# Long convolution and expert layer on one core: last block's second expert product by slices of 256 channels, first loads in quarters by k, product of the spectra with a third buffer

## Chip, cores and metric

One core of one Trainium2 chip. The metric is device time in microseconds (us) of one execution. The profile of one execution gives its span, from the first to the last instruction; the device time of that execution is a little longer.

## What is computed

A sequence of 8192 tokens with 512 channels, all in float32, goes through a gated long convolution with a residual and a layer norm, and then through an expert layer with a residual and a layer norm:

```
u = x @ W_in + b_in                       # 512 -> 1536
uc = short_conv(u, short_w, short_b)      # three taps per channel
x0, x1, v = split(uc, 3)
v = v * x1                                # the gate
k = gen_filter(8192, W1 .. b3)            # a small net with sines, times exp(-t * delta)
v = causal_fft_conv(v, k, filter_bias)    # rfft of both, product, irfft
y = (v * x0) @ W_out + b_out
x = layernorm(x + y)

logits = grouped @ controller + tie       # groups of 32 tokens, 32 experts, 4 sets
perm = (logits == max over the group's tokens)
dispatched = einsum(bgtd,bgtes->bgesd)
inner = relu(einsum(bgesd,desf->bgesf) + bias)      # f = 32
intermediate = einsum(bgesf,esfd->bgesd)            # the second expert product
out = einsum(bgesd,bgtes->bgtd)                     # back to the tokens
x = layernorm(x + out)
```

## The kernel before

**Stages.** `project` computes u, the short convolution and the gate, and the filter taps beside it; `convolve` does the long convolution as a Fourier transform written as matrix products; `experts` does the output projection, the first norm, the expert layer and the second norm. A scheduler orders the instructions of each engine by an estimate and puts in the waits; in `experts` TensorE's order is the one written down.

**Projection.** Tokens are taken in 16 blocks of 512 (`xt`, four tiles of 128 input channels, index k), output channels in four tiles `ct`, each with three streams s (x0, x1, v). `load_win(0)` (L153) brings the first channel tile's weights with one DMA per k, then `load_tokens(0)` (L158) brings `xt` with one DMA of 1 MB; SyncE issues both, and after them the small tables and the other channel tiles' weights. `projection` (L244) runs for each s four products over k into one PSUM bank (L256); ScalarE evicts the bank (L259) and VectorE goes on.

**Convolution.** It runs for each of four channel tiles: `over_n1` for taps and gate; `over_n2` (L360), whose 32 groups of four k1 values each make a PSUM tile `px` of two banks and multiply the spectra of taps and gate; `back_over_k2` (L395), 16 groups of four channels into a PSUM tile `pz` of two banks; `back_over_k1` (L415), products `py`. The product of the spectra is: ScalarE copies the taps' half of px to `hs` (L381), VectorE makes two products of 128x512 (`t`, L384, and `hs` in place, L388), and GpSimd subtracts and adds (L392, L393) into the spectrum. `hs` and `t` have two buffers each. The first product of `back_over_k2` needs all 32 groups. Each pz tile is copied by VectorE (L413) and ScalarE (L411) into `z`, and the first py product needs all of z.

**Experts.** Four blocks of 2048 tokens, each in two halves u. `front` makes projection, norm and choice of the next block, piece by piece between other work; `dispatch` and `inner` make the inner activations `h`. `outer` (L672) makes the second product for a half u and 128 channels c: eight expert groups q, four sets s and four quarters r, each a product with 32 rows, 32 columns and 128 channels (`pi`, L691), into pairs of PSUM banks; weights come in DMAs of 512 KB into six buffers `f`; ScalarE copies each pair (L700) into a staging tile, and VectorE turns it by 32x32 blocks (L704, two per call of `outer`). `back` (L710) multiplies the turned tile with the choice (`pc`, L716, 32 calls) and VectorE adds to the residual `x1` (L721). `finish` (L734) makes the second norm of a half: statistics and root on VectorE, normalisation on ScalarE (L760) and stores. In the last half of the last block, statistics are taken per 128 channels right after each addition (L729). PSUM has four pairs (`pair`), tag `x1` has four buffers of 16 KB per partition, tag `big` two of 32 KB.

The loop of the last part calls `outer` for (u, c), and after the next `outer` the `back` of the one before:

```
for u in range(2):
    for c in range(NCT):
        outer(b, u, c, [0]) ...
        turned = outer(b, u, c, [1]) ...
        if last:
            back(*last)
        if u == 1 and c == 0:
            ends = finish(b, 0)
        if u == 1:
            some(ends, 3)
        last = (b, u, c, turned)
```

Of the kernel before, what the change touches and what calls it, by code (L numbers as in the profile page):

```python
# [13 lines left out]
F32 = mybir.dt.float32  # L14
# [18 lines left out]
R = 4  # L33
EQ = E // R
EPS = 1e-5

# [107 lines left out]
def project(tc, i, bank, load, between, kept):  # L144
# [4 lines left out]
    with tc.tile_pool(name="pr1", bufs=1) as hp, tc.tile_pool(name="pr2", bufs=2) as wk:  # L149
# [14 lines left out]

        load_win(0)
        xt = load_tokens(0)
        pe = load(hp, "pe")
# [76 lines left out]
        def projection(b, ct):  # L244
            u = wk.tile([P, 3, TB + 2], F32, tag="u", name=f"u_{ct}_{b}")
            nc.gpsimd.tensor_copy(u[:, :, 0:2], carry[:, ct])
            got = []
            for s in range(3):

# [3 lines left out]

                ps = bank(f"pu_{ct}_{b}_{s}")
                for k in range(NCT):
                    nc.tensor.matmul(  # L256
                        ps, win[ct][:, k, s, :], xt[:, k, :], start=(k == 0), stop=(k == NCT - 1)
                    )
                nc.scalar.activation(u[:, s, 2:], ps, AF.Identity, bias=ch(0))  # L259
                o = wk.tile([P, TB], F32, tag=f"o{s}", name=f"o{s}_{ct}_{b}")  # L260
# [55 lines left out]
def convolve(tc, i, banks, kept, wk, tables, between, y_dram):  # L316
# [9 lines left out]
    with tc.tile_pool(name="cv", bufs=1, reuse_waits="tile") as hp:  # L326
# [33 lines left out]
        def over_n2(ct, both, of_taps, spec):  # L360
            for g in range(N1 // KC):
# [8 lines left out]
                for j in range(KC):  # L370
# [8 lines left out]

                hs = wk.tile([P, 2, 64, KC], F32, tag="hs", name="hs" + nm)  # L380
                nc.scalar.copy(hs, ps[:, :, of_taps].rearrange("p j r c -> p r c j"))  # L381
                d = ps[:, :, 1 - of_taps].rearrange("p j r c -> p r c j")
                t = wk.tile([P, 2, 64, KC], F32, tag="t", name="t" + nm)
                nc.vector.tensor_tensor(  # L384
                    t, d, hs[:, 0:1].to_broadcast([P, 2, 64, KC]), ALU.mult
                )

                nc.vector.tensor_tensor(  # L388
                    hs, d, hs[:, 1:2].to_broadcast([P, 2, 64, KC]), ALU.mult
                )  # L390
                o = spec[:, :, :, g * KC : (g + 1) * KC]
                nc.gpsimd.tensor_tensor(o[:, 0], t[:, 0], hs[:, 1], ALU.subtract)  # L392
                nc.gpsimd.tensor_tensor(o[:, 1], t[:, 1], hs[:, 0], ALU.add)  # L393

        def back_over_k2(ct, spec):  # L395
            for c0 in range(0, 64, CB):
                ps = banks(f"pz_{ct}_{c0}").rearrange("p (h c n) -> p h c n", h=2, c=CB)
                for c in range(CB):
                    for r in range(2):
                        for h in range(2):  # L400
# [5 lines left out]
                            )  # L406
                for h in range(2):
                    o = z[:, :, h * 64 + c0 : h * 64 + c0 + CB]
                    v = ps[:, h].rearrange("p c n -> p n c")
                    if h:  # L410
                        nc.scalar.copy(o, v)  # L411
                    else:
                        nc.vector.tensor_copy(o, v)  # L413

# [43 lines left out]
def experts(tc, i, load, ident, y_dram, out):  # L458
# [11 lines left out]
    with (  # L470
# [239 lines left out]
        def back(b, u, c, turned):  # L710
# [11 lines left out]
            if very_last(b, u):  # L722
# [5 lines left out]
                for t in range(HT):  # L728
                    nc.vector.bn_stats(b.st[:, t, c, :], x1[:, t, :])  # L729

        def very_last(b, u):
            return b.n == NBLK - 1 and u == 1
# [67 lines left out]
        for b in blocks:  # L800
# [23 lines left out]
            ]  # L824
            for u in range(2):
                for c in range(NCT):
                    fa, amid, fb, behind = slots[u * NCT + c]
                    outer(b, u, c, [0])
                    fa(amid)
                    turned = outer(b, u, c, [1])  # L830
                    fb(behind)
# [7 lines that stand above are left out]
# [7 lines left out]
            else:  # L846
                back(*last)
            ends = finish(b, 1)
# [3 lines left out]
def laid_out(a):  # L852
# [13 lines left out]
    for h in range(2):  # L866
# [23 lines left out]

        "f2": m["f2"].reshape(R, EQ // 2, 2, S, F, NCT, P).transpose(5, 1, 0, 4, 2, 3, 6)
        .reshape(NCT, EQ // 2, P, 2 * S * P),
        "ebias": m["bias"].reshape(R, EQ, S, F).transpose(0, 3, 1, 2).reshape(P, EQ * S),
    }
# [19 lines left out]
```

## Time and profile before

| | |
|---|---|
| device time, median of 3 runs | 2342.98 us (2339.41 to 2345.3) |
| profiled execution, device time | 2338.82 us |
| its span | 2337.0 us |
| TensorE busy | 2160.5 us (92%) |
| VectorE, ScalarE, GpSimd busy | 1288.6, 822.6, 479.4 us |
| granted TensorE clock, mean of the span | 0.966 |

The profile names a group by line, engine, operation, and tile (written<-read). PE is TensorE's products, PEld its weight loads, DVE is VectorE, ACT ScalarE, POOL GpSimd, SPq SyncE's DMA issues. A line of the timeline has start, length, engine, line, operation, tiles, shape and count, and in brackets how long the engine had been idle and what ended that. "issue" there is a wait for nothing that the profile shows. In the view of stretches each engine has its busy time and, in brackets, its number of instructions; the clock is the share of TensorE's full speed that was granted. The costliest groups of the page that concern the places above:

```profile
L691 PE MATMUL pi<-f,h 32*32 32x128 f32 x8192 | 140.8, 297 | 51.0 <-issue 29.3
...
L402 PE MATMUL pz<-c_back_sb,place 64*128 64x128 f32 x2048 | 124.7, 284 | 19.0 <-POOL place L392 19.0
```

Columns: busy time and mean ns of one, then idle time before the group and what ended most of it.

### The profile page before, as it was taken

To read this page: it belongs to the slowest core of one execution; us is meant where nothing else is said; L and a number is where in the kernel's file an instruction comes from. 1 tells how busy PE (TensorE), PEld (TensorE's weight loads), DVE (VectorE), ACT (ScalarE), POOL (GpSimd) and SP (SyncE) were. 2 spreads that over 40 slices of the span, in tenths; PEclk is the share of its full clock that TensorE was granted. 3 is DMA by queue.
4 is the path that set the end of the run, shared out by engine and by line. 5 is a ranking of instruction groups with operands and counts; after the bars stand their busy time and mean duration, and the time that the engine had idled before them with its cause. 6 is when DMAs were issued, how large, how long until landed. Compare 5 with 4: busy or idle time off the path is not lost.

```text
span 2337.0 us, 67762 instructions
## 1 busy us (share of the span) xinstructions
PE 2160.5 (92%) x30688; PEld 1487.9 (64%) x30688; DVE 1288.6 (55%) x1852; ACT 822.6 (35%) x1240; POOL 479.4 (21%) x583
## 2 busy tenths in 40 slices
PE   8999999999999999999999998889988999898765
PEld 3444444444446999999999998355555556555644
DVE  4777654454554553453463463466566666656546
ACT  4444555555553321321321321121342243234323
POOL 1111233333331340240250160211101100110000
PEclk9999999999999999999999999999998999899887
DMA  4222224231324645655554564426654664665364
GB/s 144 81 68 65 83 64 162 86 139 59 140 63 164 207 170 193 198 190 186 189 206 172 173 239 159 153 82 208 207 178 142 227 203 131 200 200 182 118 228 147
DMA packets 197016, 362.74 MB, mean 155 GB/s; under 512 B 79084, under 2 KB 118898, under 8 KB 193650
## 3 DMA queue, kind: packets, MB, share of 16 engines
q1 hardware_dynamic: 194424, 341.63, 44.4%
q10 hardware_dynamic: 2304, 16.78, 1.8%
q8 instruction: 241, 3.95, 0.7%
q14 instruction: 47, 0.39, 0.0%
HBM read 274.47 MB, written 83.89 MB: 153 GB/s over the span
## 4 chain that ended last, share of the span: by engine, by line
PE 77%; DVE 9%; ACT 5%; issue 3%; POOL 3%; DMA 1%; SPq 0%; ACTq 0%; POOLq 0%; DVEq 0%
PE pu L256 29%; PE pa L349 9%; PE po L537 8%; PE pz L402 5%; PE py L427 5%; PE pi L691 4%; PE pc L716 3%; PE px L373 3%; PE pl L574 3%; PE pd L621 3%; PE ph L654 2%; POOL place L392 2%; DVE si L704 2%; ACT x L760 2%; POOL place L393 2%
## 5 line engine op out<-in xcount | busy, mean ns | idle before, releaser
L256 PE MATMUL pu<-xt,win 128*128 128x512 f32 x1536 | 673.7, 596 | 11.0 <-DMA xt<-in_xT 11.0
L256 PEld LDWEIGHTS pu<-xt,win 128*128 128x128 f32 x1536 | 289.3, 190 | 370.1 <-issue 349.7
L262 DVE SCALAR_TENSOR_TENSOR o<-u,chan_sb,o 128x512 f32<-128x512 f32 x192 | 144.8, 754 | 296.4 <-ACT o L261 295.5
L537 PE MATMUL po<-wout,yt 128*128 128x512 f32 x512 | 241.8, 616 | 19.7 <-DVE x L541 18.5
L373 PE MATMUL px<-place,tab 128*64 128x128 f32 x4096 | 227.6, 273 | 2.1 <-ACT place L356 1.5
L373 PEld LDWEIGHTS px<-place,tab 128*64 128x64 f32 x4096 | 226.1, 136 | 3.1 <-ACT place L356 2.2
L349 PE MATMUL pa<-c_in_sb,vk 128*64 128x128 f32 x4096 | 224.9, 273 | 2.2 <-ACT place L356 1.6
L349 PEld LDWEIGHTS pa<-c_in_sb,vk 128*64 128x64 f32 x4096 | 223.5, 137 | 3.8 <-ACT place L356 1.8
L700 ACT COPY si<-pi 128x1024 f32<-128x1024 f32 x128 | 123.8, 1013 | 258.3 <-PE pi L691 179.8
L535 POOL TENSOR_TENSOR xt<-xt,b_outb_sb 128x512 f32<-128x512 f32 x64 | 82.4, 1288 | 619.0 <-DMA xt<-in_x 550.8
L704 DVE STREAM_TRANSPOSE si<-si 128x2048 f32<-128x2048 f32 x64 | 144.2, 2289 | 113.0 <-ACT si L700 113.0
L259 ACT ACTIVATE u<-pu,chan_sb 128x512 f32<-128x512 f32 x192 | 130.8, 681 | 188.1 <-PE pu L256 186.4
L392 POOL TENSOR_TENSOR place<-t,hs 128x256 f32<-128x256 f32 x128 | 93.6, 732 | 473.9 <-DVE hs L388 404.6
L691 PE MATMUL pi<-f,h 32*32 32x128 f32 x8192 | 140.8, 297 | 51.0 <-issue 29.3
L537 PEld LDWEIGHTS po<-wout,yt 128*128 128x128 f32 x512 | 94.8, 195 | 131.0 <-issue 96.8
L691 PEld LDWEIGHTS pi<-f,h 32*32 32x32 f32 x8192 | 106.9, 107 | 92.9 <-issue 54.6
L261 ACT ACTIVATE o<-u,chan_sb 128x512 f32<-128x512 f32 x192 | 155.7, 812 | 6.6
L358 DVE COPY place<-pa 128x1024 f32<-128x1024 f32 x64 | 78.3, 1225 | 139.7 <-PE pa L349 135.2
L356 ACT COPY place<-pa 128x1024 f32<-128x1024 f32 x64 | 64.7, 1013 | 251.6 <-PE pa L349 245.6
L402 PE MATMUL pz<-c_back_sb,place 64*128 64x128 f32 x2048 | 124.7, 284 | 19.0 <-POOL place L392 19.0
L402 PEld LDWEIGHTS pz<-c_back_sb,place 64*128 64x128 f32 x2048 | 123.2, 199 | 20.6 <-POOL place L392 19.9
L231 ACT ACTIVATE ex<-delta_sb,negt_sb 128x128 f32<-128x128 f32 x256 | 87.6, 390 | 133.0 <-POOL taps L238 133.0
(79 smaller groups left out, 2532.2 us busy)
## 6 DMA issues: line engine op xcount, KB each, us to landing
f<-in_f SPq DMA_DIRECT2D x192, 512.0 KB, 5.1
tab<-in_c_mid SPq DMA_DIRECT2D x64, 512.0 KB, 3.7
place<-in_c_out SPq DMA_DIRECT2D x64, 512.0 KB, 4.9
xt<-in_xT SPq DMA_DIRECT2D x16, 1024.0 KB, 5.4
x<-o SPq DMA_DIRECT2D x64, 256.0 KB, 2.4
gate<-gate SPq DMA_DIRECT2D x64, 256.0 KB, 2.6
taps<-taps SPq DMA_DIRECT2D x4, 4096.0 KB, 11.2
vk<-taps SPq DMA_DIRECT2D x32, 512.0 KB, 3.8
```

Source lines behind the costliest of these rows:

```text
L256: nc.tensor.matmul(ps, win[ct][:, k, s, :], xt[:, k, :], start=(k == 0), stop=(k == NCT - 1))
L259: nc.scalar.activation(u[:, s, 2:], ps, AF.Identity, bias=ch(0))
L261: nc.scalar.activation(o, u[:, s, 2:], AF.Identity, bias=ch(1), scale=ch(4))
L262: nc.vector.scalar_tensor_tensor(o, u[:, s, 1 : 1 + TB], ch(3), o, ALU.mult, ALU.add)
L349: nc.tensor.matmul(ps[r * 64 : (r + 1) * 64, c * N1 : (c + 1) * N1], vk[:, half * 8 + c, :], cin[:, r, :], start=True, stop=True,)
L373: nc.tensor.matmul(ps[h * 64 : (h + 1) * 64, j, :, r, :], tab[:, g % 2 * KC + j, r * 64 : (r + 1) * 64], both[:, :, g * KC + j, h * 64 : ( ...
L392: nc.gpsimd.tensor_tensor(o[:, 0], t[:, 0], hs[:, 1], ALU.subtract)
L402: nc.tensor.matmul(ps[:, h, c, :], spec[rows, r, c0 + c, :], cback[rows, r].rearrange("p q n -> p (q n)"), start=(r == 0), stop=(r == 1),)
L537: nc.tensor.matmul(ps, got["y"][:, ct, t % 2 * P : (t % 2 + 1) * P], wout[:, ct, :], start=(ct == 0), stop=(ct == NCT - 1),)
L691: nc.tensor.matmul(pss[r // 2][s * T : (s + 1) * T, col : col + P], b.h[rows, at + q, s, u * T : (u + 1) * T], f2[rows, q, s, :], start=Tr ...
L700: nc.scalar.copy(o, pss[rr].rearrange("p (r q d) -> p r d q", r=2, q=4))
L704: nc.vector.transpose(turned[:, d].rearrange("p d g -> p (d g)"), stage[:, d].rearrange("p d e -> p (d e)"),)
```

## The change

Three places. The first weights and tokens are loaded in pairs by k, and the first channel tile's twelve products of the first token block run by k instead of by stream. The product of the spectra becomes a function with three `hs` buffers; the last of the 32 groups is done in two halves of two k1 values, with the addition on VectorE instead of GpSimd, and the last pz tile is copied in two halves. In the last block `outer` is replaced by `wide`: products over 256 channels with the weights in another layout (`f2w`, same bytes), one staging tile of 256 channels, and two turned tiles per call from the buffers of tag `x1`; the two `back` of a call run after the next call.

```diff
+W = 256
...
-        load_win(0)
-        xt = load_tokens(0)
+
+        xt = wk.tile([P, NCT, TB], F32, tag="xt", name="xt_0")
+        for k in range(NCT):
+            nc.sync.dma_start(
+                out=win[0][:, k],
+                in_=i["W_in"].rearrange("(k p) (s t c) -> k t p s c", p=P, s=3, c=P)[k, 0],
+            )
+            nc.sync.dma_start(out=xt[:, k], in_=i["xT"][k * P : (k + 1) * P, 0:TB])
...
+            pss = [bank(f"pu_{ct}_{b}_{s}") for s in range(3)]
+            steps = [(s, k) for s in range(3) for k in range(NCT)]
+            if b == 0 and ct == 0:
+                steps.sort(key=lambda sk: sk[1])
+            for s, k in steps:
+                nc.tensor.matmul(
+                    pss[s], win[ct][:, k, s, :], xt[:, k, :], start=(k == 0), stop=(k == NCT - 1)
+                )
             for s in range(3):
...
-                ps = bank(f"pu_{ct}_{b}_{s}")
-                for k in range(NCT):
-                    nc.tensor.matmul(
-                        ps, win[ct][:, k, s, :], xt[:, k, :], start=(k == 0), stop=(k == NCT - 1)
-                    )
-                nc.scalar.activation(u[:, s, 2:], ps, AF.Identity, bias=ch(0))
+                nc.scalar.activation(u[:, s, 2:], pss[s], AF.Identity, bias=ch(0))
...
-                hs = wk.tile([P, 2, 64, KC], F32, tag="hs", name="hs" + nm)
...
+                n = 2 if g == N1 // KC - 1 else 1
+                for j0 in range(0, KC, KC // n):
+                    product(ps[:, j0 : j0 + KC // n], of_taps, spec, g * KC + j0, n == 2, nm)
+
+        def product(ps, of_taps, spec, k1, short, nm):
+
+            kc = ps.shape[1]
+            hs = wk.tile([P, 2, 64, kc], F32, tag="hs", name=f"hs{nm}_{k1}", bufs=3)
+            nc.scalar.copy(hs, ps[:, :, of_taps].rearrange("p j r c -> p r c j"))
+            d = ps[:, :, 1 - of_taps].rearrange("p j r c -> p r c j")
+            t = wk.tile([P, 2, 64, kc], F32, tag="t", name=f"t{nm}_{k1}")
+            nc.vector.tensor_tensor(t, d, hs[:, 0:1].to_broadcast([P, 2, 64, kc]), ALU.mult)
+
+            nc.vector.tensor_tensor(hs, d, hs[:, 1:2].to_broadcast([P, 2, 64, kc]), ALU.mult)
+            o = spec[:, :, :, k1 : k1 + kc]
+            nc.gpsimd.tensor_tensor(o[:, 0], t[:, 0], hs[:, 1], ALU.subtract)
+            add = nc.vector if short else nc.gpsimd
+            add.tensor_tensor(o[:, 1], t[:, 1], hs[:, 0], ALU.add)
...
-                for h in range(2):
-                    o = z[:, :, h * 64 + c0 : h * 64 + c0 + CB]
-                    v = ps[:, h].rearrange("p c n -> p n c")
...
+                n = 2 if c0 == 64 - CB else 1
+                for c1 in range(0, CB, CB // n):
+                    for h in range(2):
+                        at = h * 64 + c0 + c1
+                        o = z[:, :, at : at + CB // n]
+                        v = ps[:, h, c1 : c1 + CB // n].rearrange("p c n -> p n c")
...
+        def wide(b, u, c):
+
+
+            stage = wk.tile([P, W, T], F32, tag="big", name=f"sw_{b.n}_{u}_{c}")
+            for q0 in range(0, EQ, 2):
+                pss = [pair(f"pw_{b.n}_{u}_{c}_{q0}_{rr}") for rr in range(2)]
+                for q in range(2):
+                    f2 = wk.tile([P, S, W], F32, tag="f", name=f"f2_{b.n}_{u}_{c}_{q0 + q}", bufs=6)
+                    nc.sync.dma_start(
+                        out=f2.rearrange("p s d -> p (s d)"), in_=i["f2w"][c, q0 + q]
+                    )
+                    for s in range(S):
+                        for r in range(R):
+                            rows = slice(r * F, (r + 1) * F)
+                            col = r % 2 * 512 + q * W
+                            nc.tensor.matmul(
+                                pss[r // 2][s * T : (s + 1) * T, col : col + W],
+                                b.h[rows, q0 + q, s, u * T : (u + 1) * T], f2[rows, s, :],
+                                start=True, stop=True,
+                            )
+                for rr in range(2):
+                    o = stage.rearrange("p d (r q) -> p r d q", r=R)[
+                        :, 2 * rr : 2 * rr + 2, :, q0 : q0 + 2
+                    ]
+                    nc.scalar.copy(o, pss[rr].rearrange("p (r q d) -> p r d q", r=2, q=2))
+            got = []
+            for half in range(2):
+                turned = wk.tile([P, P, T], F32, tag="x1", name=f"tw_{b.n}_{u}_{c}_{half}", bufs=4)
+                for d0 in range(0, P, 64):
+                    nc.vector.transpose(
+                        turned[:, d0 : d0 + 64].rearrange("p d g -> p (d g)"),
+                        stage[:, half * P + d0 : half * P + d0 + 64].rearrange("p d e -> p (d e)"),
+                    )
+                got.append((b, u, 2 * c + half, turned))
+            return got
...
-            for u in range(2):
+            for u in range(2 if ahead else 0):
...
             else:
-                back(*last)
+                before = []
+                for u in range(2):
+                    for c in range(D // W):
+                        slices = wide(b, u, c)
+                        for last in before:
+                            back(*last)
+                        if u == 1 and c == 0:
+                            ends = finish(b, 0)
+                        some(ends, 4)
+                        before = slices
+                for last in before:
+                    back(*last)
             ends = finish(b, 1)
...
+        "f2w": m["f2"].reshape(R, EQ, S, F, D // W, W).transpose(4, 1, 0, 3, 2, 5)
+        .reshape(D // W, EQ, P, S * W),
```

The layout of `f2w` is made on the input before the launch, as that of `f2` is.

More of the change, by code (lines that the diff above doesn't have):

```diff
@@ L378, in over_n2 @@
                             )
-                hs = wk.tile([P, 2, 64, KC], F32, tag="hs", name="hs" + nm)
[L381 to L393, printed above, removed]
+                n = 2 if g == N1 // KC - 1 else 1
[13 more added lines that the diff above has]
+            add.tensor_tensor(o[:, 1], t[:, 1], hs[:, 0], ALU.add)
         def back_over_k2(ct, spec):
@@ L406, in back_over_k2 @@
                             )
-                for h in range(2):
-                    o = z[:, :, h * 64 + c0 : h * 64 + c0 + CB]
-                    v = ps[:, h].rearrange("p c n -> p n c")
[L410 to L413, printed above, removed]
+                n = 2 if c0 == 64 - CB else 1
[4 more added lines that the diff above has]
+                        v = ps[:, h, c1 : c1 + CB // n].rearrange("p c n -> p n c")
+                        if h:
+                            nc.scalar.copy(o, v)
+                        else:
+                            nc.vector.tensor_copy(o, v)
         def back_over_k1(ct, x0, tabs):
```

## The prediction

> **What bounds the kernel now.** I read the page first (TensorE busy 92% of 2337.0 us, 77% of the chain that ended last), then the busy time by stage, then the timeline at the three places that the diff touches.
>
> ```profile
> 0.00:24.00 24.00, 13.00 (x25) 5.74 (x26) 2.09 (x4) 4.22 (x6) 1.02 (x9) 1.00 0.79 225
> 24.00:730.00 706.00, 706.00 (x2055) 320.03 (x2054) 407.06 (x619) 366.12 (x652) 213.24 (x252) 1.00 0.29 96
> 730.00:1451.00 721.00, 692.04 (x11265) 687.10 (x11264) 341.12 (x418) 178.85 (x258) 182.74 (x258) 0.98 0.56 187
> 2230.00:2337.00 107.00, 68.08 (x2574) 48.40 (x2563) 63.95 (x100) 39.70 (x46) 0.00 (x0) 0.81 0.52 176
> ```
>
> Length, then busy us of PE, PEld, DVE, ACT, POOL, then granted clock, DMA share, GB/s. The projection (24 to 730) has no idle TensorE, so time saved ahead of it moves everything. The convolution has 29 us of TensorE idle. In the last 107 us no engine is full: that stretch is latency. First loads, in the timeline of the start:
>
> ```profile
> 0.74 2.66 SPq L156 DMA_DIRECT2D win<-in_W_in  x4
> 3.44 0.61 SPq L160 DMA_DIRECT2D xt<-in_xT  x1
> 11.00 23.11 PE L256 MATMUL pu<-xt,win 128*128 128x512 f32 x48 [11.00 <-DMA xt<-in_xT]
> ```
>
> The first product waits for the whole of xt. End of the products of the spectra, channel tile 0, and end of the step back over k2, in the timeline:
>
> ```profile
> 847.03 0.59 ACT L381 COPY hs<-px 128x512 f32<-128x512 f32 x1 [0.91 <-POOL place L393]
> ...
> 847.64 0.69 DVE L384 TENSOR_TENSOR t<-px,hs 128x512 f32<-128x512 f32 x1
> ...
> 848.37 0.69 DVE L388 TENSOR_TENSOR hs<-px,hs 128x512 f32<-128x512 f32 x1
> 849.14 0.72 POOL L392 TENSOR_TENSOR place<-t,hs 128x256 f32<-128x256 f32 x1
> ...
> 849.92 6.28 PE L402 MATMUL pz<-c_back_sb,place 64*128 64x128 f32 x60 [4.07 <-POOL place L392]
> ```
>
> ```profile
> 881.48 0.69 DVE L413 COPY place<-pz 128x512 f32<-128x512 f32 x1 [1.09 <-PE pz L402]
> 882.21 0.59 ACT L411 COPY place<-pz 128x512 f32<-128x512 f32 x1 [1.15 <-DVE place L413]
> 882.85 1.38 PE L427 MATMUL py<-place 128*128 128x128 f32 x10 [1.41 <-ACT place L411]
> ```
>
> px ended at 845.86, yet ScalarE took its last copy at 847.03: it waited for an hs buffer, which POOL still read. The last block, in the timeline and in the list of DMA queues from 2219 to 2300:
>
> ```profile
> 2233.19 2.87 PE L691 MATMUL pi<-f,h 32*32 32x128 f32 x127 [1.19 <-issue]
> ...
> 2237.26 2.88 PE L691 MATMUL pi<-f,h 32*32 32x128 f32 x128 [1.20 <-issue]
> ...
> 2240.32 4.50 DVE L704 STREAM_TRANSPOSE si<-si 128x2048 f32<-128x2048 f32 x2 [8.11 <-ACT si L700]
> 2241.35 2.88 PE L691 MATMUL pi<-f,h 32*32 32x128 f32 x127 [1.21 <-issue]
> ```
>
> ```profile
> DMA  9996868778787771277770796352878506965418
> GB/s 338 336 310 261 253 273 247 271 239 261 233 285 227 271 257 73 30 251 257 243 281 0 206 301 265 71 212 24 287 249 271 223 6 208 318 239 136 160 28 338
> ...
> q8 instruction: 18, 0.29, 1.5%
> ```
>
> A matmul call is two records with a weight load each (2048 pi records for 1024 calls). Bursts of 128 records begin every 4.07 us although a record follows the last after 14 ns, and no tile or buffer is named: "issue". 128 records with their loads are 256 instructions, and q8 brings 16 KB at that pace (packets at 2230.88, 2234.85, 2239.03, 2243.09).
>
> **The Trainium skill.** "Runtime: NRT & Kernel Launch", Instruction fetch mechanics: instructions arrive in blocks of 16 KiB, 256 each, and the fetch is mostly hidden. The blocks agree; hidden it is not, 4.07 us per block against some 2.5 of work. "TensorE: Matmul & The Clock Gate", Part 3: 32x32 tiles run side by side, up to 16. The pi records 13.5 to 14.5 ns apart, at granted clocks of 0.5 and 1.0 alike, fit that. The same page, Part 1: after an idle window of about 3.4 us the clock is halved. The trace's clock record shows 0.5 for 3.4 to 6.8 us after each of the four px to pz gaps. "PSUM — Partial Sum Buffer", PSUM bank collisions: engines must not touch one bank at once; here readers of one PSUM tile take turns (ACT at 882.21 after DVE ended at 882.17).
>
> **Part 1, first loads by k.** The same 1.8 MB in eight issues; the last lands near 10.8, as now. The first pair is 0.46 MB: transfer starts at 2.2, at the window's 225 GB/s it takes 2.0, with 0.6 to the semaphore 4.8 us. The 24 records then run with the first 5 or 6 at the 0.855 us of a cold clock (before: 11.00 to 15.40) and the rest at 0.43: 4.8 + 5.5 x 0.855 + 18.5 x 0.43 = 17.5. The fourth pair is there at 10.8, when record 9 runs. Before, record 25 began at 23.65: -6.1. SP has three issues more (some 2 us), which pushes win1; in the trace win1 is down at about 14.6, so about 16.6, ahead of 17.5. The order by k fills three banks together, so ScalarE gets three evictions at once; its work per channel tile (3 x (0.68 + 0.81) = 4.5) hides beside TensorE's 10.3 (24 x 0.43). Behind it the projection stays bound by TensorE, so nothing eats the gain before 730 us. I take -6.0; ends -4 and -6.5.
>
> **Part 2, products of the spectra.** With two hs buffers the loop copy 0.59, two products 1.4, two POOL passes 1.47, handovers 0.17 is 3.63 per two groups, 1.81 each; TensorE needs 57.27 / 32 = 1.79. So the lag grows and the gap px to pz (start to start) is 4.34, 4.59, 5.45, 5.68 in the four channel tiles. A third buffer ends that loop; the t buffers still bind DVE to POOL, 3.0 per two groups, which is covered. The halves of the last group do not overlap as one would like: in the built order the first copy waits for all of px_31, the second for the first half's DVE products. From px's end E: copy 0.05 to 0.42 (half of 0.59 with its fixed part), products to 0.88 and 1.34, second copy to 1.74, its products to 2.25 and 2.71, POOL subtraction to 3.2; DVE's addition is done by 3.0. pz starts at E + 3.25, 3.52 start to start. Saved: 0.8 + 1.05 + 1.9 + 2.15 = -5.9. The slow clock after the gaps costs 8.3 (pz takes 31.25, 30.3, 31.1, 30.9 against 512 x 56.3 ns = 28.8); an idle of 3.25 will mostly still trip it, since it tripped in a window that was a quarter busy: -2, ends 0 and -8. The split of the last pz copies costs: the first waits for the whole group, and the four then take turns, 0.43 + 0.37 + 0.43 + 0.37 and three handovers, 1.7 against 1.31: +0.4 x 4 = +1.6. On SP and DMA the small expert tables move ahead of yt; xt is issued 0.8 earlier behind the y stores: -0.8, where TensorE stood 10.3 us.
>
> **Part 3, the last block.** I call "slice" what one pass of the new function makes: 256 channels of one token half, four in all. 512 calls of 256 columns for 1024 of 128: 8 fetch blocks for 16, so 8.1 us per slice (2 x 4.07) for 16.3. The 256-column record isn't in the trace: if all 16 tiles run side by side its group of 64 takes 0.9 us, at half clock 1.7. Copies (0.97), transposes (2.25), pc (3.7) and bytes stay. What takes over, by two mechanisms.
>
> DMA: six tiles are ahead at 2230; the sixth lands at 2233.9 and later ones each 1.55 us (338 GB/s at 99% busy, the same DMA list's top), so slice 2 ends at 2233.9 + 10 x 1.6 + 0.6 = 2250.5 instead of 2246.4.
>
> Waits: turned tiles share four x1 buffers, two of which hold x1, so slice 2's transposes wait for the pc of slice 1 that frees them. And DVE is in order: all four transposes of a slice stand ahead of the two additions (1.2 each) that free the pc's PSUM pairs, for which the third group of the next slice waits on TensorE. The clock runs so: slice 2 ends 2250.5; first pc 2254.2; four transposes (4 x 2.27) 2263.3; additions 2265.7; slice 3's last two groups 2268.7; pc 2272.4; transposes 2281.5; additions 2283.9; statistics of half 0, 5.9, and its root, 1.7 (as at 2287.46 to 2293.38 and 2326.72 to 2328.39 now), 2291.5. In the built order four ScalarE normalisations (2.9) stand ahead of slice 4's last two copies: 2294.4, 2296.4. Transposes 2305.4; 31 small statistics (0.205) and three additions, 10.0, 2315.4. Behind the last statistics the trace has 2337.0 - 2325.7 = 11.3: end 2326.7. So of 32 us of fetch 10.3 remain. Ends: -3 (DMA at the 255 GB/s of now, and slow records) and -15 (statistics overlap).
>
> **Sum.** -6.0 - 5.9 - 2 + 1.6 - 0.8 - 10.3 = -23.4 of a profiled execution of 2338.8 (span 2337.0). The runs' median is 2343.0, so 2319 to 2320; I say 2319.
>
> **Rivals.** A, the forecast, 2319. B, no gain at the end: transposes and DMA eat it all, because DVE idles while a slice fills and all four transposes follow; DVE's 64 of 107 us busy speak against it, the "waits" above for it: 2330. C, the clock stays up after px and the tail overlaps better: -8 for -2, -15 for -10: 2308. D, slower: a 256-column record occupies its row group for its whole stream, so only four tiles work at a time. py gives 112 ns per 128 columns: 225 / 4 = 56 ns at full clock, 75 at 0.75. 768 records of the chain above at 75 are 57.6 for 25.8, +32: 2351. It decides from about 72 ns per record. Against it: 13.5 ns at half clock needs all 16. E, the first loads gain nothing because quarter transfers are paced by SP: 2325.
>
> **Chances.** A 0.53, B 0.15, C 0.13, D 0.06, E 0.13. Between 2305 and 2334 lie A, most of C, B and E. A measurement of this kernel can tell 0.3%, 7 us, from no change. Faster 0.86 (A, C, E, most of B), same 0.07 (B with a gap cost unimproved, mild D), slower 0.07 (D).
>
> **What would show it.** First matmul near 5 us; px to pz gaps all near 3.5; pz to py 2.1; pw bursts of 128 records 4 us apart or held by f; TensorE idle in slices 3 and 4 put down to the x1 additions. The forecast is wrong if pw records lie over 50 ns apart, if the first matmul stays beyond 8 us, or if slice 4's copies end after 2305.

## The result, and the profile after

The changed kernel takes 2323.31 us (median of 4 runs, 2319.64 to 2328.02) beside 2341.82 for the kernel before in the same runs: ratio 0.9921, 95% interval 0.9896 to 0.9946, which is 18.5 us (12.6 to 24.4) less. The profiled execution took 2320.76 us with a span of 2319.0; before, 2338.82 and 2337.0. The forecast was 2319, in a range of 2305 to 2334.

The changed kernel by stretches, in the same view as before (length, busy us of PE, PEld, DVE, ACT, POOL, then granted clock, DMA share, GB/s):

```profile
0.00:18.00 18.00, 13.17 (x26) 5.84 (x27) 0.00 (x0) 3.34 (x5) 1.02 (x9) 1.00 0.79 212
18.00:724.00 706.00, 706.00 (x2055) 319.84 (x2053) 410.22 (x622) 366.47 (x654) 213.53 (x252) 1.00 0.30 98
724.00:1441.00 717.00, 690.42 (x11263) 686.42 (x11262) 346.58 (x438) 179.81 (x266) 181.34 (x258) 0.99 0.57 188
2218.00:2319.00 101.00, 63.20 (x1573) 38.13 (x1572) 64.00 (x100) 40.26 (x46) 0.00 (x0) 0.80 0.53 189
```

The projection has the same length, 706 us without an idle TensorE, and begins 6 us sooner. The convolution is 4 us shorter and the last block 6 in these whole microseconds (3.5 and 6.6 in the table of the experiments). In the last block TensorE executes 1000 records less, but VectorE's 64 us are what they were.

The start, in the timeline of the changed kernel:

```profile
0.74 0.69 SPq L169 DMA_DIRECT2D win<-in_W_in  x1
1.48 0.58 SPq L173 DMA_DIRECT2D xt<-in_xT  x1
2.12 0.57 SPq L169 DMA_DIRECT2D win<-in_W_in  x1
...
4.83 11.76 PE L260 MATMUL pu<-xt,win 128*128 128x512 f32 x22 [4.83 <-DMA xt<-in_xT]
```

The first product starts at 4.83 for 11.00, after one pair of quarters. The end of the products of the spectra in channel tile 0, where px ends at 839.55:

```profile
839.63 0.37 ACT L398 COPY hs<-px 128x256 f32<-128x256 f32 x1 [1.16 <-PE px L383]
...
840.56 0.42 DVE L403 TENSOR_TENSOR hs<-px,hs 128x256 f32<-128x256 f32 x1
...
841.02 0.60 DVE L407 TENSOR_TENSOR place<-t,hs 128x128 f32<-128x128 f32 x1
841.07 0.37 ACT L398 COPY hs<-px 128x256 f32<-128x256 f32 x1 [1.07 <-DVE hs L403]
...
841.55 0.42 DVE L401 TENSOR_TENSOR t<-px,hs 128x256 f32<-128x256 f32 x1
842.01 0.42 DVE L403 TENSOR_TENSOR hs<-px,hs 128x256 f32<-128x256 f32 x1
...
842.51 0.56 POOL L405 TENSOR_TENSOR place<-t,hs 128x128 f32<-128x128 f32 x1 [0.58 <-DVE hs L403]
843.12 1.66 PE L416 MATMUL pz<-c_back_sb,place 64*128 64x128 f32 x12 [3.58 <-POOL place L405]
```

ScalarE no longer waits for a buffer: its copy begins 0.08 us after px's end. But the second half's copy starts only at 841.07, when VectorE is done with the first half, so the two halves stand one after the other: 3.58 us of idle TensorE for 4.07. The last block:

```profile
2222.95 4.21 PE L763 MATMUL pw<-f,h 32*32 32x256 f32 x127 [2.18 <-issue]
...
2229.03 6.97 PE L763 MATMUL pw<-f,h 32*32 32x256 f32 x199 [1.87 <-issue]
...
2236.27 0.73 PE L763 MATMUL pw<-f,h 32*32 32x256 f32 x32 [0.27 <-DMA f<-in_f2w]
2238.00 0.69 PE L763 MATMUL pw<-f,h 32*32 32x256 f32 x23 [1.01 <-DMA f<-in_f2w]
2240.93 1.83 PE L763 MATMUL pw<-f,h 32*32 32x256 f32 x41 [2.24 <-issue]
2242.69 7.19 PE L733 MATMUL pc<-tw,permT 128*32 128x128 f32 x128
...
2246.51 8.89 DVE L777 STREAM_TRANSPOSE tw<-sw 128x2048 f32<-128x2048 f32 x4 [4.62 <-issue]
...
2255.33 2.31 DVE L738 TENSOR_TENSOR x<-pc,x 128x1024 f32<-128x1024 f32 x2
...
2257.70 4.07 PE L763 MATMUL pw<-f,h 32*32 32x256 f32 x124 [0.51 <-DVE x L738]
...
2284.14 2.93 ACT L813 ACTIVATE x<-x,nm,rs 128x512 f32<-128x512 f32 x4 [1.28 <-DVE nm L806]
...
2286.97 1.92 ACT L772 COPY sw<-pw 128x1024 f32<-128x1024 f32 x2
...
2288.92 8.89 DVE L777 STREAM_TRANSPOSE tw<-sw 128x2048 f32<-128x2048 f32 x4 [2.45 <-ACT sw L772]
```

In slices 1 and 2 TensorE stands three times for what the profile calls issue (2.18, 1.87 and 2.24 us) and twice for a tile f (0.27 and 1.01); the end of slice 2, at 2242.76, comes after the last of these stalls. From there the chain is the one forecast: four transposes, both additions behind them, TensorE's last groups behind the additions, and for slice 4 two copies behind four normalisations.

Between the first record of `po` and the last block lie three expert blocks whose own instructions no part changes. They take 779.0 us before, 777.3 in the changed kernel.

### The profile page after: what moved, and what is told of

It is laid out like the page before. It is cut to its first block, busy times and chain, and to the rows that moved or that the text cites. A ratio compares the mean times of both kernels' runs of the same rounds, so it can differ in the third digit from the quotient of the medians.

```text
span 2319.0 us, 65860 instructions
## 1 busy us (share of the span) xinstructions
PE 2152.6 (93%) x29664; PEld 1474.7 (64%) x29664; DVE 1297.3 (56%) x1872; ACT 823.7 (36%) x1248; POOL 478.2 (21%) x583
## 5 line engine op out<-in xcount | busy, mean ns | idle before, releaser
L717 ACT COPY si<-pi 128x1024 f32<-128x1024 f32 x96 | 93.0, 1012 | 196.6 <-PE pi L708 138.3
L721 DVE STREAM_TRANSPOSE si<-si 128x2048 f32<-128x2048 f32 x48 | 108.1, 2290 | 85.0 <-ACT si L717 85.0
L416 PE MATMUL pz<-c_back_sb,place 64*128 64x128 f32 x2048 | 123.6, 284 | 14.8 <-POOL place L405 14.8
L708 PE MATMUL pi<-f,h 32*32 32x128 f32 x6144 | 103.4, 291 | 30.2 <-issue 18.2
L398 ACT COPY hs<-px 128x512 f32<-128x512 f32 x132 | 75.5, 572 | 156.9 <-PE px L383 149.0
```

Of the source, the lines that this page charges most:

```text
L416: nc.tensor.matmul(ps[:, h, c, :], spec[rows, r, c0 + c, :], cback[rows, r].rearrange("p q n -> p (q n)"), start=(r == 0), stop=(r == 1),)
L708: nc.tensor.matmul(pss[r // 2][s * T : (s + 1) * T, col : col + P], b.h[rows, at + q, s, u * T : (u + 1) * T], f2[rows, q, s, :], start=Tr ...
L717: nc.scalar.copy(o, pss[rr].rearrange("p (r q d) -> p r d q", r=2, q=4))
L721: nc.vector.transpose(turned[:, d].rearrange("p d g -> p (d g)"), stage[:, d].rearrange("p d e -> p (d e)"),)
```

## Experiments

Device time says little about effects of some us: the runs of one kernel spread over 7 to 21 us. So each kernel was also profiled, and the lengths below are counted in its trace from first record to first record: "start" up to the first px, "convolution" from there to the first `po`, "blocks" the three expert blocks, "last" from the last block's first record of the second product to the end. The gap is from the last px record's start to the first of pz, and "pz" the stage from its first to its last record, for the four channel tiles.

| kernel | ratio to before (95%) | start | convolution | blocks | last | gaps px to pz | pz |
|---|---|---|---|---|---|---|---|
| before | | 788.5 | 662.7 | 779.0 | 106.9 | 4.34, 4.59, 5.45, 5.68 | 31.2, 30.3, 31.1, 30.9 |
| changed | 0.9921 (0.9896 to 0.9946) | 782.2 | 659.2 | 777.3 | 100.3 | 3.85, 3.89, 3.90, 4.25 | 31.2, 30.2, 30.2, 30.9 |
| e1_loads | 0.9971 (0.9958 to 0.9985) | 783.0 | 663.3 | 779.2 | 107.3 | 4.31, 4.65, 5.47, 5.58 | 31.6, 30.5, 31.1, 31.0 |
| e2_spectra | 0.9998 (0.9986 to 1.001) | 789.2 | 659.8 | 785.3 | 106.5 | 3.85, 3.89, 3.90, 4.37 | 31.5, 30.2, 30.2, 30.8 |
| e3_wide | 0.9978 (0.9968 to 0.9988) | 789.9 | 663.3 | 788.2 | 97.5 | 4.35, 4.65, 5.41, 5.64 | 31.5, 30.4, 31.1, 31.0 |
| e4_third | 0.9968 (0.9957 to 0.998) | 790.3 | 656.1 | 785.7 | 108.8 | 3.32, 3.32, 3.38, 3.38 | 31.6, 30.7, 30.7, 30.5 |
| f0_base | 0.9904 (0.9885 to 0.9922) | 783.2 | 653.5 | 778.8 | 98.6 | 3.31, 3.31, 3.38, 3.38 | 30.4, 30.5, 30.5, 29.0 |
| f1_order | 0.9883 (0.9865 to 0.9901) | 782.8 | 655.8 | 785.9 | 92.2 | 3.31, 3.31, 3.38, 3.38 | 30.5, 30.5, 30.5, 31.7 |
| g1_fill | 0.9843 (0.9824 to 0.9862) | 782.6 | 649.5 | 768.9 | 98.5 | 3.32, 3.32, 3.38, 3.38 | 29.0 in all |
| g2_half | one run | 781.5 | 658.5 | 778.9 | 93.2 | 3.85, 3.89, 3.89, 4.37 | 28.6, 31.5, 30.2, 31.0 |
| h1_best | 0.9825 (0.9805 to 0.9846) | 781.9 | 649.4 | 778.8 | 89.4 | 3.32, 3.32, 3.39, 3.38 | 29.0 in all |
| h2_fill12 | one run | 782.4 | 651.9 | 780.0 | 98.1 | 3.31, 3.31, 3.38, 3.38 | 29.0, 30.7, 29.0, 30.7 |

The column "blocks" is a warning: the same work took from 768.9 to 788.2 us from one execution to the next. What moves it no run here shows. A difference of a single profile is read from the other columns only.

**One part at a time: e1_loads, e2_spectra, e3_wide.** Each is the kernel before with one of the three hunks of the change and nothing else.

> The kernel before with the first loads by k alone. My theory: all of the 6.3 us that the first px record comes earlier in the changed kernel (788.47 to 782.16) is this part, and nothing after it takes it back: 6.3 us faster than before (ratio 0.9973), with the experts' last block at 106.9 us as before. Rival: the small stall that opens the projection is only moved, and the first loads give back some of it at the next wait for a DMA (win1, the first token tiles): 3 us or less.

Measured: 6.8 us less (3.5 to 9.8), the first px record 5.5 us earlier in its trace. All executions with the new loads have a start of 781.5 to 783.2, all without of 788.5 to 790.3. The theory stands: nothing in the projection eats the gain.

> The kernel before with the product of the spectra as in the changed kernel alone (third hs buffer, halves of the last group with an addition on VectorE, split last pz copies). My theory, from the gaps of the changed kernel: px to pz starts 3.85 to 4.25 us apart (before 4.34 to 5.68), pz to py 2.07 (before 1.69), so 3.5 us faster in the convolution, and about 1.6 more up to the last block because the small expert tables are issued ahead of the first yt tiles: 3.5 to 5 us in all (ratio 0.998 to 0.9985). Rival: the gain at the experts' start belongs to another part, then 3.5 and no more.

Measured: no difference in device time (3.3 us less to 2.3 more), 2.9 us less in the convolution by the trace. The interval leaves out the theory's 3.5 to 5 us in all, and just leaves out the 3.5 of the rival too; the convolution's 2.9 lie inside it. The 1.6 us at the experts' start are not confirmed: TensorE's waits at `po` there are 12.4 us in all for 13.4 before, but 13.7 in the changed kernel, and the spread of the blocks hides what is that small.

> The kernel before with the last block's second product by slices of 256 channels alone. My theory: the last block takes 100.3 us as in the changed kernel for 106.9, so 6.6 us faster (ratio 0.9972), and the first two slices again end about 23 us after the first pw record. Rival: the 23 us for 20 of the forecast come from where the block begins in the stream of instructions (blocks of 256 instructions start elsewhere here), then slices 1 and 2 end at another time by up to 2 us and the gain is between 5 and 9.

Measured: 5.2 us less (2.8 to 7.5), the last block 97.5 us, slices 1 and 2 over 22.9 us after the first pw record. The gain in time and the end of the slices agree with the theory; the block's length does not, but it differs from one execution to the next. Over all five profiled executions that have this last block (changed, e3_wide, f0_base, g1_fill, h2_fill12) it is 98.6 on average, over the four with the old one (before, e1_loads, e2_spectra, e4_third) 107.4. So the block is 8.8 us shorter by the traces, more than the 6.6 of the first two profiles. The 5.2 us of device time (at most 7.5) are less than that, and where the rest goes no run shows. Nor does a run separate, within part 3, the fewer calls from the order and the buffers that come with them.

The three parts alone add up to 12.4 us of device time, with an error of some 5, beside 18.5 (12.6 to 24.4) for the whole change. The two can be the same within the noise; no run shows that the parts help each other.

**The third buffer without the halves: e4_third.** One argument is added to the kernel before:

```diff
-                hs = wk.tile([P, 2, 64, KC], F32, tag="hs", name="hs" + nm)
+                hs = wk.tile([P, 2, 64, KC], F32, tag="hs", name="hs" + nm, bufs=3)
```

> The kernel before with a third hs buffer alone: the last group of px is not split, POOL keeps both passes and the last pz copies stay whole. My theory: the halves take turns on ScalarE and VectorE and so gain nothing; with the whole group the chain is copy 0.6, two products 1.4, POOL's subtraction 0.75 and handovers 0.3, so the gap px to pz is 3.3 to 3.6 us in all four channel tiles, pz to py stays 1.69, and the convolution is 5.5 to 7 us shorter (ratio 0.997), more than with the whole of part 2. Rival: the halves do shorten the chain; then the gap is above 4.25 us here and the convolution gains less than 3.5 us.

Measured: 7.5 us less (4.7 to 10.1), the convolution 6.6 shorter, the gaps 3.32 to 3.38, and pz to py again 1.68. The rival falls. The timeline of e4_third at tile 0, px's end at 847.70:

```profile
847.78 0.59 ACT L381 COPY hs<-px 128x512 f32<-128x512 f32 x1 [1.16 <-PE px L373]
...
848.47 0.69 DVE L384 TENSOR_TENSOR t<-px,hs 128x512 f32<-128x512 f32 x1 [0.33 <-ACT hs L381]
...
849.20 0.69 DVE L388 TENSOR_TENSOR hs<-px,hs 128x512 f32<-128x512 f32 x1
849.97 0.72 POOL L392 TENSOR_TENSOR place<-t,hs 128x256 f32<-128x256 f32 x1 [0.34 <-DVE hs L388]
...
850.74 2.13 PE L402 MATMUL pz<-c_back_sb,place 64*128 64x128 f32 x14 [3.04 <-POOL place L392]
```

Four instructions and four handovers (the time from one engine's end to the next one's start) make 3.04 us of idle time, half a microsecond less than the two halves with seven instructions in a row. One line of part 2 has all the gain, and the other lines give part of it back: 0.5 to 0.9 us per tile in the gap, 0.39 per tile at pz to py. The device times agree: the intervals of e4_third and e2_spectra do not meet. In tile 0 the halves lose because the second copy waits for VectorE's reading of the first half. The two halves lie in different banks of px, but in one PSUM tile; whether two halves in PSUM tiles of their own would run side by side, no run tried.

**The changed kernel with that line alone for part 2: f0_base.**

> The changed kernel with the third hs buffer kept, but the last group of px whole, both its passes on GpSimd and the last pz copies whole (part 2 reduced to one buffer). From the third buffer alone (gap px to pz 3.32 to 3.38, pz to py 1.68) and the changed kernel (3.85 to 4.25 and 2.07): 3.5 us less in the convolution, everything else as in the changed kernel, so about 22 us faster than before, ratio 0.9905. Rival: in the changed kernel something else paid for the halves (the clock in pz is a little higher there, 30.2 for 30.7 us), then no difference to the changed kernel's 0.992.

Measured: ratio 0.9904 for 0.9921, and by the trace a convolution 5.7 us shorter than the changed kernel's. The intervals of the two ratios overlap; the stage's length decides it. Of the 5.7, 2.1 are pz (122.5 to 120.4 over the four tiles) and were not expected: in the last channel tile the clock did not fall, and pz took 29.04. That is explained below.

**The order of the last block: f1_order.** On f0_base, `wide` gets the two pending `back` and puts one ahead of its third group and one between the two halves of the transposes:

```diff
             for q0 in range(0, EQ, 2):
+                if q0 == 4 and before:
+                    back(*before[0])
                 pss = [pair(f"pw_{b.n}_{u}_{c}_{q0}_{rr}") for rr in range(2)]
...
             for half in range(2):
+                if half and before:
+                    back(*before[1])
                 turned = wk.tile([P, P, T], F32, tag="x1", name=f"tw_{b.n}_{u}_{c}_{half}", bufs=4)
```

> f0_base with another order of the last block: the two pc of a slice no longer follow all groups of the next slice, the first goes after its second group, the second after its fourth, and each addition to x1 goes ahead of the transposes that follow it on VectorE. My theory: slices 3 and 4 are held by the chain transposes, pc, additions, last groups, copies, 19 us per slice; with the new order the additions no longer wait for four transposes, so a slice takes 13 to 15 us, slice 4's last copies no longer stand behind four normalisations, and the last block is 8 to 12 us shorter than 100.3: ratio 0.986 to 0.987. Rival: VectorE's own work (transposes 8.9, additions 2.4, statistics) or the loads of the tiles set the pace anyway, then 3 us or less.

Measured: the block 92.2 us, 6.4 less than f0_base's and 8.1 less than the changed kernel's; the ratio 0.9883 is short of the 0.986 to 0.987 expected, and its interval overlaps f0_base's, so that the gain is shown by the block's length in one profile (the five of the old order are 97.5 to 100.3). The mechanism is there for slice 3. Slices 2, 3 and 4 begin their transposes 15.1, 14.6 and 22.7 us after the one before, where the changed kernel has 13.5, 19.0 and 23.4: slice 4 hardly gained. Its lines in the timeline of f1_order:

```profile
2277.01 1.98 ACT L766 COPY sw<-pw 128x1024 f32<-128x1024 f32 x2 [3.06 <-PE pw L757]
...
2278.66 1.46 PE L757 MATMUL pw<-f,h 32*32 32x256 f32 x60 [1.46 <-DVE x L730]
...
2283.51 0.21 ACT L506 ACTIVATE rt<-ve 128x8 f32<-128x8 f32 x1 [4.52 <-DVE ve L505]
2283.63 1.00 ACT L766 COPY sw<-pw 128x1024 f32<-128x1024 f32 x1
...
2285.11 2.93 ACT L809 ACTIVATE x<-x,nm,rs 128x512 f32<-128x512 f32 x4 [0.48 <-DVE nm L802]
2287.94 0.99 ACT L766 COPY sw<-pw 128x1024 f32<-128x1024 f32 x1
2288.97 4.50 DVE L773 STREAM_TRANSPOSE tw<-sw 128x2048 f32<-128x2048 f32 x2 [1.47 <-ACT sw L766]
```

TensorE's last products were done near 2280, but ScalarE stood 4.52 us at the root of the first half's norm (L506), and both copies were queued behind it, one of them behind four normalisations too. The scheduler orders VectorE and ScalarE, and it had put the root there.

**Filling the gap: g1_fill and h2_fill12.** On f0_base, after the last px group:

```diff
+            ps = banks(f"fill_{ct}").rearrange("p (j s r c) -> p j s r c", j=KC, s=2, r=2)
+            for n in range(28):
+                j, r, h = n // 4 % 4, n // 2 % 2, n % 2
+                nc.tensor.matmul(
+                    ps[h * 64 : (h + 1) * 64, j, :, r, :], tab[:, j, r * 64 : (r + 1) * 64],
+                    both[:, :, j, h * 64 : (h + 1) * 64], start=True, stop=True,
+                )
```

> f0_base with 28 further calls of the px form, into a PSUM tile that nobody reads, between the last px group and the first of pz (3.1 us of TensorE work in a gap of 3.35). My theory of the clock term of the prediction: the idle gap is what halves the granted clock at the start of pz; kept busy, pz takes 28.8 to 29.2 us for 30.5 to 31.6 in each channel tile and the kernel is 5 to 8 us faster than f0_base. Rival: the throttle follows something else than this gap, then pz stays at 30.2 to 31.6 and the kernel is the same as f0_base or up to 1 us slower.

Measured: pz 29.04 us in all four channel tiles, with the gaps as long as in f0_base. The convolution in the view of stretches:

```profile
724.00:1441.00 717.00, 700.53 (x11499) 692.70 (x11497) 342.76 (x419) 178.59 (x258) 182.86 (x258) 1.00 0.58 191
```

The fill in the timeline of g1_fill at tile 0:

```profile
839.81 3.27 PE L407 MATMUL fill<-place,tab 128*64 128x128 f32 x53
...
843.07 0.49 PE L419 MATMUL pz<-c_back_sb,place 64*128 64x128 f32 x4
```

The granted clock is 1.00 over the whole convolution; the clock record has no entry of 0.5 from 10.2 to 1440.4 us of the span. The theory stands and the rival falls. The convolution is 4.0 us shorter than in f0_base, where one tile had escaped by luck, and 9.7 shorter than in the changed kernel. In device time the kernel gained 14 us (ratio 0.9843 for 0.9904), more than the 5 to 8 expected, though the two intervals lie only some 5 us apart. Between the two profiled executions, 9.9 us of the gain lie in the blocks, which took only 768.9 us in this profile and 778.8 in h1_best with the same fill. I take that for their spread, not for an effect of the fill; no run settles it.

> g1_fill with 12 further calls (1.35 us of TensorE work) for 28 (3.1 us), so that some 2.0 us of the gap px to pz stay idle. My theory: it is the length of the idle stretch that counts, and 2 us is short enough: the clock stays at 1.0 and pz takes 29.04 us in every channel tile as with 28 calls. Rival: any idle of that size costs in proportion, then pz takes 29.6 to 30.5 in at least two tiles.

Measured: 29.04, 30.67, 29.04, 30.67. The theory falls: an idle stretch of 1.73 to 1.79 us is short enough in two tiles and too long in two. A cost in proportion, the rival, would not be nothing in two tiles, so it falls too.

**Half the loads: g2_half.** In `wide` of the changed kernel, every second load is left out, and each tile serves two expert groups:

```diff
                 for q in range(2):
-                    f2 = wk.tile([P, S, W], F32, tag="f", name=f"f2_{b.n}_{u}_{c}_{q0 + q}", bufs=6)
...
+                    if q == 0:
+                        f2 = wk.tile([P, S, W], F32, tag="f", name=f"f2_{b.n}_{u}_{c}_{q0 + q}", bufs=6)
```

> The changed kernel with every second load of a weight tile left out in the last block's second product: each tile is used for two experts' slots (so the output of the last block is not that of the reference), 16 loads of 512 KB for 32. My theory of the first two slices: the sixteenth tile lands 19.6 us after the first pw record, as forecast, and a fetch of instructions and the last records follow one after the other; with half the loads the landing goes and only the fetch of 256 instructions per 4.07 us is left: slices 1 and 2 end 16.5 to 18.5 us after the first pw record for 23.5 to 24, and the block is 4 to 5 us shorter. Rival: the stalls called issue in these slices are the instruction fetch alone and loads do not matter: 22 us or more, and the block as long as before.

Measured: slice 2's last copies begin 18.3 us after the first pw record (2218.83) for 24.1 in the changed kernel, and the block takes 93.2 for 100.3 (97.5 at the least in the other executions with this order). TensorE in these slices, in the timeline of g2_half:

```profile
2222.00 3.27 PE L764 MATMUL pw<-f,h 32*32 32x256 f32 x106 [0.21 <-issue]
...
2227.02 2.84 PE L764 MATMUL pw<-f,h 32*32 32x256 f32 x107 [0.78 <-issue]
...
2231.31 3.04 PE L764 MATMUL pw<-f,h 32*32 32x256 f32 x108 [0.48 <-issue]
...
2235.79 1.30 PE L764 MATMUL pw<-f,h 32*32 32x256 f32 x41 [0.45 <-issue]
```

No wait for a tile f is left (1.3 us in the changed kernel), the stalls called issue ahead of a burst are 0.2 to 0.8 us, 1.9 in all, for 1.87 to 2.24, 6.3 in all, and bursts of 127 records begin 4.3 to 5.0 us apart. So the loads cost slices 1 and 2 some 5.8 us, and the rival falls. How they lengthen the stalls called issue is shown only in part: ahead of the first two of the changed kernel no tile was waited for. With half the loads the DMA engines were also less busy in these slices (0.71 for 0.93) and the granted clock was higher (0.93 for 0.76), and no run separates the three. The gain was larger than the 4 to 5 us expected: slice 2 brings 5.8 of it, and slice 3 begins its transposes 17.7 us after slice 2 for 19.0.

**The version that beats both: h1_best.** It is g1_fill with f1_order's order, the order of VectorE and ScalarE in the last block written out too, statistics taken per slice, and the first half's root put behind slice 4's copies:

```diff
                 if q0 == 4 and before:
                     back(*before[0])
+                    parts(2)
...
                 if half and before:
+                    if u == 1 and c == 1:
+                        some(finish(b, 0), 99)
                     back(*before[1])
```

`parts(n)` takes the statistics of the n oldest pending pairs of half and 128 channels.

> g1_fill (first loads by k, third buffer alone, 28 further calls between px and pz, slices of 256 channels) with the last block's order of f1_order, written out for VectorE and ScalarE too: the statistics of both token halves are taken per slice and stand in the 3.7 us in which VectorE waits for the last groups, and the first half's root and normalisations come after slice 4's last copies. From f1_order: slices start their transposes 14.6 to 15 us apart, but slice 4 only 22.7 after slice 3. My theory: that one also comes down to 15 to 17, so the last block takes 84 to 87 us for 98.5 and 92.2, and the kernel is 11 to 14 us faster than g1_fill: ratio 0.978 to 0.980. Rival: VectorE's summed work is then the bound (17 us per slice with statistics) and the block takes 90 us or more, ratio 0.981 or above.

Measured: 2300.04 us, ratio 0.9825 (0.9805 to 0.9846), the last block 89.4 us. That is 41 us less than before and clearly less than the changed kernel; against g1_fill the intervals overlap, and the block's 9 us less are shown by the profile alone. The expectation of 84 to 87 us and 0.978 to 0.980 was missed; the ratio is in the rival's range and the block just short of its 90. In its timeline:

```profile
2268.06 4.50 DVE L790 STREAM_TRANSPOSE tw<-sw 128x2048 f32<-128x2048 f32 x2 [0.96 <-ACT sw L781]
...
2275.10 0.17 DVE L819 SCALAR_TENSOR_TENSOR nm<-mv,rs 128x8 f32<-128x8 f32 x1
2275.19 1.22 DVE L738 TENSOR_TENSOR x<-pc,x 128x1024 f32<-128x1024 f32 x1
2276.32 4.49 DVE L790 STREAM_TRANSPOSE tw<-sw 128x2048 f32<-128x2048 f32 x2
```

The slices now start 13.7, 15.5 and 16.1 us apart, but the root's 2.7 us, which I had let ScalarE's copies go ahead of, stand between slice 4's own transposes on VectorE. They were moved from one queue on the chain to another. The rival's mechanism is there too: from 2236.5 to 2284.0, slices 2 to 4, VectorE is busy for 44.0 of 47.5 us (in the changed kernel for 48.5 of the 64.8 from slice 1's transposes to slice 4's end). So from slice 2 on its summed work is nearly the bound, and what a better order could still gain there is at most the 3.5 us in which it is idle.

## Why the prediction was right, and where its sum was not

The total was forecast at -23.4 and came out at -18.5 (-12.6 to -24.4). Term by term, with what the trace and the single parts gave:

| term of the sum | forecast | measured |
|---|---|---|
| first loads | -6.0 (-4 to -6.5) | -6.3 in the two first profiles; alone, in device time, -6.8 (-3.5 to -9.8) |
| gaps px to pz | -5.9 | -4.2 |
| clock in pz | -2 (0 to -8) | -1.0 |
| split pz copies | +1.6 | +1.5 |
| small tables on SyncE | -0.8 | no gain shown: waits at `po` at the experts' start 13.7 us for 13.4, the longest 9.7 for 10.3 |
| last block | -10.3 (-3 to -15) | -6.6 in the two first profiles, -8.8 over nine; alone, in device time, -5.2 (-2.8 to -7.5) |

By the two first profiles these terms make 16.6 us; another 1.6 of the 18.1 by which they differ lie in the blocks, which is spread and no merit of the change.

*First loads.* Right with its mechanism: 4.83 for a first product forecast at 4.8, and rival E (no gain) falls.

*The gaps.* I forecast 3.52 us in all tiles, and they are 3.85 to 4.25. I had seen that the halves take turns, but in the chain of the second half I put its copy at 1.74 us and its products right behind, up to 2.71 after px's end. In the trace of tile 0 these are at 1.89 and 2.88, and the first of pz at 3.57 for 3.25: I had added durations and left out most handovers, 0.03 to 0.1 us each at seven places, and GpSimd's half pass takes 0.56. In tile 3 VectorE was still at group 30 when px ended, and the gap is 4.25. The larger lapse was one of comparison: the same durations, added up for an undivided group, give 0.59 + 2 x 0.69 + 0.72 and handovers, some 3.0, and I never made that sum. e4_third did.

The turns of VectorE and ScalarE that the prediction set beside PSUM bank collisions are no case of them: in the kernel the two copies of pz read different banks, so what is seen is the order of the built program.

*The clock.* The step "an idle of 3.25 will mostly still trip it" held, but then -2 was too much: of the seven windows of half clock before, six were left. g1_fill shows what there was to be had, 7.4 us (123.6 to 116.2 over the four pz stages), and that idle time must go, not shrink.

*The last block.* D falls, by far: at full clock the first 33 pw records of a burst follow each other after 13.4 to 14.3 ns, counted from the trace's starts, like those of pi. Over more records they are slower than I took them: a group of 64 takes 1.1 us for the forecast's 0.9 (2249.81 to 2250.93), and at half clock they lie 25 to 27 ns apart (from 2258.35). My reading that pi records lie 13.5 to 14.5 ns apart at both clocks was too smooth as well: over a whole burst it is 14 at full clock (109 records from 2251.12 in the trace of before) and 19 at half (127 from 2233.19).

The forecast's chain from slice 2 on holds nearly to the microsecond: from slice 2's transposes at 2246.51 to slice 4's at 2288.92 are 42.4 us, and the forecast had 2254.2 to 2296.4, 42.2. What was mis-sized is the end of slice 2. I put it at the last tile's landing plus 0.6. By the semaphore events in the trace of the changed kernel (the signals that a transfer has landed), which the waits for the two tiles before bear out, the sixteenth tile landed at 2239.24, 20.6 us after the first pw record; the forecast had 19.8, and the expectation of g2_half has 19.6, which is too early. But the slice ended at 2242.76, 3.5 after it. TensorE waited for the fifteenth tile until 2238.00, went through 23 records and stood again until 2240.93, although the sixteenth tile came in between: the packet with the next 16 KB of instructions ran only from 2238.63 to 2239.55, after the wait. I had treated DMA and fetch as two limits of which the larger counts; here one came behind the other. That the wait held the fetch back is read from this order of events; no run shows it alone. e3_wide's end is as late with another stall before it: the sixteenth tile lands at 19.9, a packet runs to 2261.57 and the last burst begins at 2263.08, but the burst before had waited for ScalarE and not for a tile. g2_half shows that with half the loads the slice is done by 18.3.

*What carried the forecast.* The five terms that can be measured had the right sign, and the three larger ones kept their mechanism. Three of them were taken too large, by 1.7 (gaps), 1.0 (clock) and, by the first two profiles, 3.7 us (last block), and none too small by as much as 1, so no error hid another. The range was wide, though: 2305 to 2334 holds the rivals B and E and most of C as well, so that a time within it says little, and it is the single parts that bear the mechanism out. Of the rivals B (no gain at the end) falls by e3_wide. C's clock was there to be had, but not through this change.

## What to carry to other kernels

Before work is split to shorten a chain, add up the chain of the undivided work with the buffer that it lacked: here one more buffer had the whole gain, and the halves cost a part of it since in this program the readers of one PSUM tile take turns. Where TensorE must idle for a few microseconds ahead of a long stretch, ask what the idle time does to the clock afterwards; products that nobody reads can be cheaper than the wait. And look for small work of another purpose (a root, four normalisations) in the queue of an engine on the chain: an instruction that waits there holds everything behind it, and if it is moved, see which queue it lands in, and how much of that queue is still free.

## What the runs showed of the hardware that was not expected

- The clock falls by a fixed grid. Every entry of 0.5 in the convolution's clock record is 3.413 us long or twice that, and its starts lie on multiples of 3.413 us of each other. This agrees with the Trainium skill, "TensorE: Matmul & The Clock Gate", Part 1, which tells of a free-running window of that length. What these runs add is that a window need not be idle. I laid the gaps of the traces on windows of 3.413 us counted from an entry of 0.5, and took a window's busy share as what the gap leaves of it: windows busy for 0.41 or less were followed by a slow one in every case, those above 0.55 in none where the clock was full, and between the two it went either way (f0_base's last channel tile kept its clock with a gap of 3.10 us cut into two windows of 0.42 and 0.67; h2_fill12 lost it twice with 1.73 to 1.79). So the same gap costs 1.6 us or nothing, by where it falls. The way back asks for more: of the windows at half clock, those that the gap still left busy for 0.37 to 0.85 were followed by another slow one in all 17 cases, and only those without a part of the gap by full clock.
- After a stall called issue in the second product, TensorE's records begin again 1.0 to 1.6 us after a packet with 16 KB of instructions has ended, in all 15 such stalls at the beginning of the last block in four traces (before, changed, e3_wide, g2_half). The later that packet comes, the longer the stall. In the changed kernel the stalls are 2.18, 1.87 and 2.24 us, and the last follows a wait for a tile after 23 records; with half the loads they are 0.2 to 0.8.
- The same three expert blocks took between 768.9 and 788.2 us in twelve profiled executions. The cause stays open.
